# A recommendation model on one core: the product of GRU state and item moves from GpSimd to VectorE

## The chip, the cores and the metric

One core of a Trainium2 chip. The metric is the time of one execution on the device in microseconds (us), lower is better. Engines are named as the profile names them: PE (TensorE matmuls), PEld (its weight loads), DVE (VectorE), ACT (ScalarE), POOL (GpSimd), SP (SyncE, which issues most DMAs).

## The reference, cut to what matters

B = 1024 users, T = 100 history items of 128 numbers, hidden size 128, all in float32. A GRU runs over the history; an attention MLP scores each GRU state against the user's item; the scores are made a softmax over time; the pooled result weights a second recurrence (AUGRU); a last MLP gives one score a user.

```python
def gru_step(h, x_t):
    gi = x_t @ gru_Wih.T + gru_bih
    gh = h @ gru_Whh.T + gru_bhh
    r, z = sigmoid(i_r + h_r), sigmoid(i_z + h_z)
    n = tanh(i_n + r * h_n)
    return (1.0 - z) * n + z * h
keys = all the GRU states                       # B x T x 128
q = item_embedding, repeated for each t
feat = concatenate([keys, q, keys - q, q * keys], axis=-1)
score = mlp(feat, 512 -> 80 -> 40 -> 1, relu)
attn = softmax(where(mask == 1, score, -inf), axis=1)
pooled = einsum('bt,btd->bd', attn, keys)
# then: AUGRU over keys with weights from pooled, and the last MLP
```

## The kernel before, in words

The states are held transposed, 128 features on the partitions and users along the free axis. The 1024 users are two halves of 512 (`Half`), whose GRUs alternate. The first phase, `gru_phase`, loops over the 100 steps `s` and in each over the two halves. For one half it issues:

- `load(s + 2)` and `load_mask(s + 2)`: DMAs on SP, into pools of eight buffers each.
- `gru(s)`: the gate matmuls on PE (L363; each float32 matmul of 128x512 is two instructions), the sigmoids and the tanh on ACT (L375, L380, L394), and five operations on DVE: `u` (L383), the sum L393, and L396, L397, L398, the last of which writes the new state `hn`.
- `attend(s - 1)`: the first layer of the attention MLP for the state of the step before. The features `keys` and `q` are folded into the weights `wk` and into the constant `q0`; for `q * keys` the kernel forms `kq`, state times item, 128x512 (L429), in a pool `wp` of two buffers. PE multiplies `wk` by the state (L431) and `wkq` by `kq` (L432) into the same PSUM tile `pm`; DVE adds `q0` (L434, `f`), ACT applies the relu.
- `transpose(s - 1)`: four transposes on PE (L409), a copy to SBUF by ACT (L410), and every fourth step a DMA of the key tile `kt` (eight buffers).
- `attend_more(s - 1)`, once a step: the two later layers for both halves together (PE L618 into `px`, ACT L627); the scores go out by a small DMA (L445).
- `stage()`: pieces of the softmax, run in blocks of up to eight steps (PE L470, DVE L475 to L493, ACT L485).
- `history(s)`: the masked sum of the raw items, two operations on POOL (L350, L351).
- `pool(2, nc.gpsimd)`: for up to two keys of a finished softmax block, weight and add, two operations on POOL each (L525, L526), and one rescaling a block (L511).

The PSUM pool of `pm`, the transposes, `px` and softmax's scores (tag "a") has two buffers, that of the gates six. At the end of the phase come the last pooling, `weights`, `features` and `sort_weights` (L582 builds comparison masks on POOL).

The order on each engine is not simply that of the program text. The framework plans the whole phase beforehand with costs of its own: whenever an engine comes free in the plan, it takes, among the instructions whose inputs and buffers are ready in the plan, the one that comes first in the program. The order so found is fixed; on the chip each engine works through its own queue in that order and waits on semaphores.

The second phase, `augru_phase`, holds the AUGRU and the last MLP; it is planned apart from the first and has no part in the change.

Of the kernel before, what the change touches and what calls it, by code (L numbers as in the profile page):

```python
# [53 lines left out]
def kernel(ctx: ExitStack, tc: tile.TileContext, a: dict, out: bass.AP):  # L54
# [16 lines left out]
    nc = tc.nc  # L71
# [18 lines left out]
    item = const.tile([P, B], F32, name="item")  # L90
# [28 lines left out]
    def gru_phase(pools):  # L119
# [195 lines left out]
        class Half:  # L315
# [102 lines left out]
            def attend(self, t):  # L418

                i = self.i  # L420
                mv = wp.tile([P, HB], F32, name="mv", bufs=4)
                self.old, self.mv = self.mv, mv
                if t == T:
                    nc.gpsimd.memset(mv, 0.0)
                if t >= T:
                    return
                h = self.h[t]
                kq = wp.tile([P, HB], F32, name="kq")
                nc.gpsimd.tensor_mul(kq, h, item[:, self.cols])  # L429
                p = pa.tile([P, HB], F32, tag="a", name="pm")  # L430
                nc.tensor.matmul(p, lhsT=wk[i], rhs=h, start=True, stop=False)  # L431
                nc.tensor.matmul(p, lhsT=wkq[i], rhs=kq, start=False, stop=True)  # L432
                f = wp.tile([P, HB], F32, name="f")
                nc.vector.tensor_add(f, p, q0[:, self.cols])  # L434
                nc.scalar.activation(mv, f, AF.Relu)
# [453 lines left out]
```

## Time and profile before

| | us |
|---|---|
| median of three runs | 2664.23 (2659.52 to 2665.18) |
| the profiled execution's own time | 2684.05 |
| its span | 2681.6 |
| PE busy | 2434.5 (91%) |
| DVE busy | 1382.1 (52%) |
| ACT busy | 1215.7 (45%) |
| POOL busy | 1370.2 (51%) |
| GRU phase with its end | about 0 to 1912 |
| AUGRU phase | about 1912 to 2681 |

Busy shares are averages over the whole span: POOL is used mostly in the first phase. In the groups of the page, a row gives the line, the engine, the operation, what it writes and reads, shapes and count, then busy time and mean duration in ns, and last the idle time of the engine just before these instructions with what ended most of it. A timeline row gives start, duration, engine, line and operation; merged rows carry a count, and a bracket holds the idle time before and what ended it. The granted clock is the share of full speed that PE was given.

### The profile page before, as it was taken

How to read it: one execution, taken by the hardware profiler on the slowest of the kernel's cores; microseconds unless marked ns; L12 is line 12 of the kernel's file. 1: busy time of each engine (PE TensorE's matmuls, PEld its weight loads, DVE VectorE, ACT ScalarE, POOL GpSimd, SP SyncE). 2: the span in 40 equal slices, each digit the busy share in tenths (PEclk: the TensorE clock that was granted, in tenths of full speed). 3: DMA queues.
4: the chain of work that ended last, by engine and by line, in shares of the span. 5: the costliest groups of instructions: out<-in, count | busy, mean ns of one | idle time of the engine just before them, and what ended most of it. 6: DMA issues, size and time to landing. Idle time of an engine off the chain costs nothing. (4 is left out here: it accounts for less than half of the span.)

```text
span 2681.6 us, 25839 instructions
## 1 busy us (share of the span) xinstructions
PE 2434.5 (91%) x7688; PEld 1232.2 (46%) x7688; DVE 1382.1 (52%) x2530; ACT 1215.7 (45%) x2125; POOL 1370.2 (51%) x1215
## 2 busy tenths in 40 slices
PE   8999888898888888899888888897789999999998
PEld 3443333343333333344333333333444555667887
DVE  6644444544444444545444444454356666666664
ACT  3544444444444444444444444443234444455554
POOL 3457877565656767665656767667512111211220
PEclk9999999999999999999999999998799999999998
DMA  6323322212222222112222222111223233333331
GB/s 141 99 81 97 95 90 66 74 58 73 77 73 76 75 74 75 52 61 73 74 77 73 77 73 77 49 64 36 86 80 108 85 101 98 93 92 96 79 86 23
DMA packets 141655, 210.20 MB, mean 78 GB/s; under 512 B 29646, under 2 KB 75698, under 8 KB 141506
## 3 DMA queue, kind: packets, MB, share of 16 engines
q1 hardware_dynamic: 129410, 170.93, 20.7%
q0 software_dynamic: 12096, 37.54, 4.9%
q8 instruction: 62, 1.02, 0.2%
q14 instruction: 87, 0.71, 0.1%
HBM read 154.12 MB, written 53.87 MB: 78 GB/s over the span
## 5 line engine op out<-in xcount | busy, mean ns | idle before, releaser
L363 PE MATMUL ps<-x,wih 128*128 128x512 f32 x1200 | 603.2, 613 | 4.6 <-DMA x<-in_hist_x 4.6
L363 PE MATMUL ps<-hn,whh 128*128 128x512 f32 x1188 | 594.4, 609 | 0.0
L429 POOL TENSOR_TENSOR kq<-hn,item 128x512 f32<-128x512 f32 x200 | 254.5, 1278 | 559.1 <-DVE hn L398 540.5
L432 PE MATMUL pm<-kq,wkq 128*128 128x512 f32 x400 | 239.6, 684 | 190.2 <-POOL kq L429 190.1
L383 DVE SCALAR_TENSOR_TENSOR u<-ps,bhh,r 128x512 f32<-128x512 f32 x198 | 148.6, 750 | 506.2 <-ACT r L375 309.6
L101 POOL DMA_INDIRECT rows<-keys_d,idx x140 | 132.8, 949 | 535.9 <-PE pk L714 490.4
L363 PEld LDWEIGHTS ps<-hn,whh 128*128 128x128 f32 x1188 | 223.1, 195 | 326.8 <-issue 319.6
L410 ACT COPY kt<-pk 128x512 f32<-128x512 f32 x200 | 117.3, 586 | 517.2 <-PE pk L409 515.7
L363 PEld LDWEIGHTS ps<-x,wih 128*128 128x128 f32 x1200 | 221.7, 199 | 199.3 <-issue 197.9
L394 ACT ACTIVATE ps<-ps,bih 128x512 f32<-128x512 f32 x200 | 132.4, 662 | 321.6 <-DVE ps L393 317.9
L351 POOL TENSOR_TENSOR hist<-hist,xm 128x512 f32<-128x512 f32 x200 | 251.8, 1274 | 1.6
L434 DVE TENSOR_TENSOR f<-pm,q 128x512 f32<-128x512 f32 x200 | 136.7, 684 | 215.1 <-PE pm L432 215.0
L526 POOL TENSOR_TENSOR pooled<-pooled,kw 128x512 f32<-128x512 f32 x190 | 242.3, 1275 | 4.3
L350 POOL TENSOR_TENSOR xm<-x,m 128x512 f32<-128x512 f32 x200 | 229.4, 1162 | 22.9 <-DMA x<-in_hist_x 16.7
L432 PEld LDWEIGHTS pm<-kq,wkq 128*128 128x128 f32 x400 | 79.5, 210 | 300.1 <-POOL kq L429 223.6
L431 PE MATMUL pm<-hn,wk 128*128 128x512 f32 x400 | 206.9, 599 | 6.0 <-ACT kt L410 3.7
L396 DVE TENSOR_TENSOR d<-hn,ps 128x512 f32<-128x512 f32 x198 | 136.0, 687 | 138.5 <-ACT ps L394 137.6
L525 POOL TENSOR_TENSOR kw<-kt,e 128x512 f32<-128x512 f32 x190 | 196.8, 1052 | 1.7 <-DVE old L492 0.4
L409 PEld LDWEIGHTS pk<-ident,hn 128*128 128x128 f32 x800 | 112.6, 155 | 125.8 <-issue 116.8
L627 ACT ACTIVATE mv<-px,bx 41x512 f32<-41x512 f32 x202 | 137.9, 683 | 68.4 <-PE px L618 65.8
L375 ACT ACTIVATE r<-ps,brz 128x512 f32<-128x512 f32 x200 | 137.5, 688 | 67.7 <-PE ps L363 64.6
L743 DVE TENSOR_TENSOR ph<-ph,h 128x512 f32<-128x512 f32 (+22 forms) x198 | 94.6, 478 | 142.4 <-ACT ph L741 127.5
(139 smaller groups left out, 3608.7 us busy)
## 6 DMA issues: line engine op xcount, KB each, us to landing
x<-in_hist_x SPq DMA_DIRECT2D x212, 256.0 KB
keys_d<-kt SPq DMA_DIRECT2D x50, 1024.0 KB
m<-mask_d SPq DMA_DIRECT2D x200, 128.0 KB
at<-att_d SPq DMA_DIRECT2D x22, 256.0 KB
s_b<-mv SPq DMA_DIRECT2D x200, 2.0 KB
rows<-keys_d,idx POOLq DMA_INDIRECT x140
at<-att_d SPq DMA_DIRECT2D x8, 246.5 KB
at<-att_d SPq DMA_DIRECT2D x8, 236.0 KB
```

The source lines that it names most:

```text
L350: nc.gpsimd.tensor_mul(d, x, m)
L351: nc.gpsimd.tensor_add(acc, acc, d)
L363: nc.tensor.matmul(p, lhsT=w[:, g, :], rhs=v, start=(j == 0), stop=(j == len(parts) - 1),)
L375: nc.scalar.activation(r, pr, AF.Sigmoid, bias=brz[:, 0:1])
L383: nc.vector.scalar_tensor_tensor(out=u, in0=ph, scalar=bhh[:, 2:3], in1=r, op0=ALU.add, op1=ALU.mult,)
L429: nc.gpsimd.tensor_mul(kq, h, item[:, self.cols])
L431: nc.tensor.matmul(p, lhsT=wk[i], rhs=h, start=True, stop=False)
L432: nc.tensor.matmul(p, lhsT=wkq[i], rhs=kq, start=False, stop=True)
L434: nc.vector.tensor_add(f, p, q0[:, self.cols])
L525: eng.tensor_mul(d, k, w)
L526: eng.tensor_add(acc, acc, d)
L627: nc.scalar.activation(half.mv[r, :], p[r, :], AF.Relu, bias=bx[r, :])
```

## The change

`attend` forms `kq` on VectorE instead of GpSimd; nothing else in the text of the kernel differs. The planner makes its order anew.

```diff
                 h = self.h[t]
                 kq = wp.tile([P, HB], F32, name="kq")
-                nc.gpsimd.tensor_mul(kq, h, item[:, self.cols])
+                nc.vector.tensor_mul(kq, h, item[:, self.cols])
                 p = pa.tile([P, HB], F32, tag="a", name="pm")
                 nc.tensor.matmul(p, lhsT=wk[i], rhs=h, start=True, stop=False)
                 nc.tensor.matmul(p, lhsT=wkq[i], rhs=kq, start=False, stop=True)
```

## The prediction

> **What bounds the kernel now.** I read the page first (shares of the engines, then the costliest groups), then PE's waits, then a timeline of a few steps, then stretches of time. Lines of the page:
>
> ```profile
> span 2681.6 us, 25839 instructions
> PE 2434.5 (91%) x7688; PEld 1232.2 (46%) x7688; DVE 1382.1 (52%) x2530; ACT 1215.7 (45%) x2125; POOL 1370.2 (51%) x1215
> L429 POOL TENSOR_TENSOR kq<-hn,item 128x512 f32<-128x512 f32 x200 | 254.5, 1278 | 559.1 <-DVE hn L398 540.5
> L432 PE MATMUL pm<-kq,wkq 128*128 128x512 f32 x400 | 239.6, 684 | 190.2 <-POOL kq L429 190.1
> ```
>
> PE is busy 91% of the span. Nearly all of its idle time in the GRU phase stands in front of one line, L432, and one releaser ends it: the product kq on POOL, 190.1 us. The next three answers are PE's waits between 139 and 1770 us, the busy times of two stretches of the GRU phase and its end, and of one period of eight steps.
>
> ```profile
> PE pm L432 <- POOL kq L429: 169.0, 33, 7.5
> 100.00:1770.00 1670.00, 1500.94 (x4035) 655.03 (x4034) 794.89 (x1265) 757.12 (x1143) 1081.18 (x928) 0.94 0.23 74
> 1770.00:1912.00 142.00, 106.84 (x337) 51.85 (x336) 72.43 (x158) 54.12 (x90) 100.65 (x85) 0.89 0.12 44
> 1165.30:1315.50 150.20, 134.81 (x361) 58.90 (x360) 71.36 (x114) 67.66 (x103) 95.61 (x83) 0.93 0.22 71
> ```
>
> In a stretch row the columns after the length are PE, PEld, DVE, ACT, POOL, granted clock, DMA. POOL is busy only 1081 of 1670 us, and it idles 540.5 us waiting for hn: it is late not for want of time, but because kq stands in its queue behind bursts of `history` and `pool` work. The timeline shows a step without and one with such a wait (start, duration; in brackets the idle time before):
>
> ```profile
> 1005.61 1.02 PE L432 MATMUL pm<-kq,wkq 128*128 128x512 f32 x2
> 1006.55 0.69 DVE L398 TENSOR_TENSOR hn<-ps,d 128x512 f32<-128x512 f32 x1
> 1007.15 0.68 DVE L434 TENSOR_TENSOR f<-pm,q 128x512 f32<-128x512 f32 x1
> 1007.38 1.28 POOL L429 TENSOR_TENSOR kq<-hn,item 128x512 f32<-128x512 f32 x1 [7.32 <-DVE hn L398]
> 1007.77 1.88 PE L363 MATMUL ps<-hn,whh 128*128 128x512 f32 x4
> 1009.75 0.75 DVE L383 SCALAR_TENSOR_TENSOR u<-ps,bhh,r 128x512 f32<-128x512 f32 x1 [1.92 <-PE ps L363]
> 1012.92 1.02 PE L432 MATMUL pm<-kq,wkq 128*128 128x512 f32 x2
> 1013.75 0.69 DVE L398 TENSOR_TENSOR hn<-ps,d 128x512 f32<-128x512 f32 x1
> 1014.36 0.68 DVE L434 TENSOR_TENSOR f<-pm,q 128x512 f32<-128x512 f32 x1
> 1015.17 1.06 PE L618 MATMUL px<-mv,w 121*41 121x512 f32 x4
> 1018.48 0.75 DVE L383 SCALAR_TENSOR_TENSOR u<-ps,bhh,r 128x512 f32<-128x512 f32 x1 [3.44 <-ACT r L375]
> 1021.95 1.02 PE L432 MATMUL pm<-kq,wkq 128*128 128x512 f32 x2
> ```
>
> ```profile
> 612.12 1.27 POOL L429 TENSOR_TENSOR kq<-hn,item 128x512 f32<-128x512 f32 x1
> 613.44 2.08 PE L432 MATMUL pm<-kq,wkq 128*128 128x512 f32 x2 [7.39 <-POOL kq L429]
> 617.58 1.88 PE L363 MATMUL ps<-hn,whh 128*128 128x512 f32 x4
> 1197.75 2.08 PE L432 MATMUL pm<-kq,wkq 128*128 128x512 f32 x2 [2.36 <-POOL kq L429]
> ```
>
> The kq made from the hn of 1006.55 is read only at 1021.95, a step later, since `attend(s-1)` follows `gru(s)`. After a wait the two L432 matmuls take 2.08 us instead of 1.02: the wait also halves PE's clock for a while (granted on average 0.94 in the long stretch). From L432 to the whh matmuls it is 4.14 us there (613.44 to 617.58) against 2.16 (1005.61 to 1007.77): 1.98 us more.
>
> **What a step is without waits, and with.** Starts of px, one per step:
>
> ```profile
> 1107.53 1.06 PE L618 MATMUL px<-mv,w 121*41 121x512 f32 x4
> 1123.33 1.06 PE L618 MATMUL px<-mv,w 121*41 121x512 f32 x4
> 1165.34 1.06 PE L618 MATMUL px<-mv,w 121*41 121x512 f32 x4
> 1315.54 1.05 PE L618 MATMUL px<-mv,w 121*41 121x512 f32 x3
> ```
>
> An unhindered step takes 15.80 us, eight of them 126.4; the eight from 1165.34 take 150.20. That is 23.8 us lost per period, of which some 15.4 are waits for kq (2.36 above is one of three) and 8.4 the slow clock and what else follows.
>
> **The change, part by part.** *Removed from POOL:* 200 products of 1.278 us, 254.5 us. POOL's own time is worth nothing; what counts is that L432 no longer stands behind POOL's queue. *The waits:* 169.0 us in the 33 cases between 139 and 1770 us go: -169.0. *The clock:* 33 x 1.98 = 65 us go with them: -65 (bounds: 0, and by the period's ratio 8.4/15.4 x 169.0 = 92). The Trainium skill, in "TensorE: Matmul & The Clock Gate", section "What's actually happening", says that the clock falls to half after an idle window of some 3.4 us and rises after as long a busy one. By that, as an estimate, a wait would cost 1.7 us, 33 of them 56, and the sum would be 2444; the row of 1197.75 disagrees with it in one point, since there 2.36 us of idling were enough. *The end:* 190.1 - 169.0 = 21.1 us of waits lie almost all after 1770, where POOL is busy 100.65 of 142 us with pooling that must be done anyway; I take -5 (bounds 0 and -21).
>
> *Added to VectorE:* 200 products of two SBUF operands. The nearest rows are the same shape on VectorE at the end of the phase, the first of these, and a small product of softmax that met a POOL operation:
>
> ```profile
> L525 DVE TENSOR_TENSOR kw<-kt,e 128x512 f32<-128x512 f32 x8 | 5.5, 685 | 1.2 <-POOL pooled L526 1.2
> 1025.65 1.06 POOL L511 TENSOR_TENSOR pooled<-pooled,e 128x512 f32<-128x512 f32 x1 [1.07 <-ACT e L485]
> 1025.72 1.01 DVE L492 TENSOR_TENSOR old<-den,e 128x4 f32<-128x4 f32 x1
> ```
>
> So 0.685 us each, 137 us in all, if nothing is in the way. L492 has four columns, yet lasts 1.01 us, to within 0.02 us of the end of POOL's L511 (1026.71): a VectorE product of two SBUF operands waits out the POOL operation that it meets. A kq may so last up to 1.28 + 0.69 = 1.97 us. Where does it stand? kq can start when hn is done (1007.24), behind f (until 1007.83), and the next VectorE work of the GRU, u, starts at 1009.75: a gap of 1.92 us; in the other half f ends at 1015.04 and u starts at 1018.48, a gap of 3.44. Free, it is hidden (0.69 of 1.92); blocked in full it makes u 0.05 us late. A late u costs little by itself: the hn that follows is read by PE a step later. Where softmax shares the gap, the slip can reach f and through it px. I take +10 us (bounds 0 and 66, below). If the gap were gone, the 137 us would come on the path. *New wait:* kq needs a buffer (two of them) that the L432 two products earlier read; that ended at 1006.63, ahead of hn. Queued behind kq on VectorE are u of the other half and softmax's small operations; PE waits for both only by way of hn and f.
>
> *Queues it is moved past:* on POOL, `history` and `pool` no longer stand behind a kq that waits for hn, so x and mask buffers are freed earlier and SyncE issues those loads at other times. POOL's load per period falls from 95.61 to 95.61 - 16 x 1.278 = 75.2 us, 59% of 127: no bound. No DMA is added or removed.
>
> **Where the planner puts it.** Lines of a queue are not in program order, as two places show (L582 belongs to `sort_weights`, the last thing in the phase):
>
> ```profile
> 1856.06 1.56 POOL L582 TENSOR_SCALAR here<-ranks,rank 128x512 f32<-128x512 f32 x1 [4.10 <-PE ps L363]
> 1020.76 0.69 DVE L396 TENSOR_TENSOR d<-hn,ps 128x512 f32<-128x512 f32 x1 [0.73 <-ACT ps L394]
> 1021.36 0.18 DVE L475 TENSOR_TENSOR e<-pt,on 128x32 f32<-128x32 f32 x1
> 1021.68 0.68 DVE L397 TENSOR_TENSOR d<-ps,d 128x512 f32<-128x512 f32 x1
> ```
>
> Work that is ready is drawn ahead, over steps of the GRU on POOL and between two steps of one GRU on VectorE. So I expect kq in VectorE's gap right after its hn, a step before PE needs it, not where the program has it, after the next hn.
>
> **The sum**, against the median 2664.2: -169.0 - 65 - 5 + 10 = -229, so 2435 us. The profiled execution took 2684.05, 0.7% above the median; its waits are used as they stand.
>
> **Rivals.**
> (a) *Slower: kq stays in program order on VectorE.* Then it starts after the hn of the next step, and L432, for which PE was ready at 1005.61, starts at 1007.24 + 0.69 = 1007.93: 2.3 us late; in the other half 1014.44 + 0.69 = 15.13 against 12.92, 2.2. That is 4.5 us a step, 450 in 100 steps, against 239 won (169 + 65 + 5): 2664 - 239 + 450 = 2875, more if such waits halve the clock as at 1197.75. It decides when over 239/2.25 = 106 of the 200 stand so. L475 and L582 speak against it; for it speaks that no row shows a VectorE instruction drawn ahead by a whole step.
> (b) *POOL blocks VectorE on the path.* POOL without kq is busy about (1081 - 226)/1670 = 51% in the long stretch (226 for kq's share, 254.5 x 1670/1880), a hit waits 0.64 us on average: 0.33 x 200 = 66 us, if all of it came on the path; 2664 - 239 + 66 = 2491. Much the same comes if kq is put ahead of f: px starts 0.13 us after f's end (1015.04), so 0.69 us a step, 69 in all. The gaps speak against both. The rule of the Trainium skill that speaks against the change is this one: "SBUF — State Buffer", section "Who interferes with whom", has VectorE with two SBUF inputs and a reading GpSimd exclude each other for a whole instruction; the row of L492 agrees.
> (c) *Another wait takes over:* x loads, whose buffers wait for `history`, or key buffers that wait for `pool`. Half of the 239 would be left: 2545. For it: POOL still works in bursts, and a faster PE asks for x sooner. Against it: PE's matmuls waited for an x only once, at the start, with POOL more loaded than it will be:
>
> ```profile
> PE ps L363 <- DMA x<-in_hist_x: 4.6, 1, 4.6
> ```
>
>
> **How the numbers follow.** Main case (2395 to 2475) 0.60; (b) 0.18; (c) 0.13, of which 0.03 with the whole gain lost; (a) 0.07; better than 2395 0.02. The low end is 2664 - 169 - 92 - 8 = 2395. The high end, 2560, takes in (b) and the half loss of (c). Faster 0.90, within 0.2% (about what a measurement of this kernel can tell from no change) 0.03, slower 0.07.
>
> **What would show it.** Right: no wait of PE at L432 worth over 20 us in all, granted clock from 100 us on near 0.99, nearly every px 15.8 to 16.4 us after the last, kq at 0.69 to 1.97 us directly behind f or hn, and the phase after the GRU unchanged at some 770 us. Wrong: L432 waiting about 2 us for VectorE in each half step (a), px waiting for f (b), or L363 waiting for x and L409 for key buffers (c).

## The result, and the profile after

The changed kernel takes 2404.24 us (median; 2402.62 to 2407.18) against 2663.4: a ratio of 0.903, interval 0.9014 to 0.9046. It is 259 us faster; 229 were forecast, and 2404 lies in the main case (2395 to 2475), at its fast end.

From the page of the changed kernel, the engines and three of the costliest groups:

```profile
PE 2349.1 (98%) x7688; PEld 1200.1 (50%) x7688; DVE 1557.9 (65%) x2730; ACT 1211.0 (50%) x2125; POOL 1173.1 (49%) x1015
```

```profile
L432 PE MATMUL pm<-kq,wkq 128*128 128x512 f32 x400 | 204.4, 592 | 0.0
L429 DVE TENSOR_TENSOR kq<-hn,item 128x512 f32<-128x512 f32 x200 | 198.4, 992 | 0.9
L351 POOL TENSOR_TENSOR hist<-hist,xm 128x512 f32<-128x512 f32 x200 | 267.2, 1351 | 2.5
```

PE's longest waits in the changed kernel (total us, count, longest):

```profile
PE px L618 <- ACT kt L410: 17.5, 14, 8.2
PE pw L589 <- DVE att L538: 11.3, 1, 11.3
```

L432 stood idle 190.1 us before and stands idle 0.0 now. VectorE is 176 us busier and POOL 197 less. The product itself lasts 0.992 us on average, not 0.685, and POOL's `history` sum 1.351 us instead of 1.274: the two engines get in each other's way. What that costs on the path is looked at below, with POOL made quiet.

The same 87 steps of the GRU phase, px to px, before and after (length, PE, PEld, DVE, ACT, POOL, clock, DMA share, GB/s):

```profile
139.20:1766.00 1626.80, 1457.74 (x3913) 636.27 (x3912) 773.52 (x1231) 733.14 (x1108) 1057.61 (x907) 0.94 0.23 74
```

```profile
129.20:1525.70 1396.50, 1388.31 (x3913) 609.32 (x3912) 932.56 (x1406) 728.11 (x1108) 890.87 (x732) 1.00 0.27 87
```

The same 3913 PE instructions take 230.3 us less. PE's idle time fell from 169.06 to 8.19 us (160.9), its busy time by 69.4 us, with the granted clock up from 0.94 to 1.00. A step (1396.5/87) takes 16.05 us, close to the 15.80 of an unhindered one: the phase is now bound by PE. The timeline of one step shows kq where it was expected:

```profile
803.68 1.02 PE L432 MATMUL pm<-kq,wkq 128*128 128x512 f32 x2
804.45 0.69 DVE L398 TENSOR_TENSOR hn<-ps,d 128x512 f32<-128x512 f32 x1
805.05 0.68 DVE L434 TENSOR_TENSOR f<-pm,q 128x512 f32<-128x512 f32 x1
805.65 0.86 DVE L429 TENSOR_TENSOR kq<-hn,item 128x512 f32<-128x512 f32 x1
805.93 1.06 PE L618 MATMUL px<-mv,w 121*41 121x512 f32 x4
809.24 0.75 DVE L383 SCALAR_TENSOR_TENSOR u<-ps,bhh,r 128x512 f32<-128x512 f32 x1 [2.72 <-ACT r L375]
812.18 1.02 PE L432 MATMUL pm<-kq,wkq 128*128 128x512 f32 x2
```

kq follows f, and VectorE still idles 2.72 us before u. PE's own order is, but for two instructions in the first steps, that of the kernel before, over all 7688.

### The profile page after: what moved, and what is told of

The parts are those of the page before. It is cut to its first block, busy times and chain, and to the rows that moved or that the text cites. A ratio compares the mean times of both kernels' runs of the same rounds, so it can differ in the third digit from the quotient of the medians.

```text
span 2400.8 us, 25461 instructions
## 1 busy us (share of the span) xinstructions
PE 2349.1 (98%) x7688; PEld 1200.1 (50%) x7688; DVE 1557.9 (65%) x2730; ACT 1211.0 (50%) x2125; POOL 1173.1 (49%) x1015
## 5 line engine op out<-in xcount | busy, mean ns | idle before, releaser
L363 PE MATMUL ps<-x,wih 128*128 128x512 f32 x1200 | 582.5, 595 | 4.2 <-DMA x<-in_hist_x 4.2
L351 POOL TENSOR_TENSOR hist<-hist,xm 128x512 f32<-128x512 f32 x200 | 267.2, 1351 | 2.5
L350 POOL TENSOR_TENSOR xm<-x,m 128x512 f32<-128x512 f32 x200 | 244.5, 1239 | 39.2 <-DMA x<-in_hist_x 34.9
L511 POOL TENSOR_TENSOR pooled<-pooled,e 128x512 f32<-128x512 f32 x25 | 26.3, 1051 | 463.2 <-ACT e L485 463.2
L526 POOL TENSOR_TENSOR pooled<-pooled,kw 128x512 f32<-128x512 f32 x190 | 247.6, 1303 | 6.6
L525 POOL TENSOR_TENSOR kw<-kt,e 128x512 f32<-128x512 f32 x190 | 209.2, 1119 | 1.8 <-DVE old L492 0.6
L432 PE MATMUL pm<-kq,wkq 128*128 128x512 f32 x400 | 204.4, 592 | 0.0
L429 DVE TENSOR_TENSOR kq<-hn,item 128x512 f32<-128x512 f32 x200 | 198.4, 992 | 0.9
L435 ACT ACTIVATE mv<-f 128x512 f32<-128x512 f32 x200 | 126.0, 630 | 114.3 <-DMA s_b<-mv 59.1
L741 ACT ACTIVATE ph<-ph,bh 128x512 f32<-128x512 f32 (+22 forms) x200 | 97.2, 486 | 125.9 <-PE ph L727 125.6
L393 DVE TENSOR_TENSOR ps<-ps,u 128x512 f32<-128x512 f32 x200 | 140.0, 700 | 20.9 <-PE ps L363 0.5
```

Of the source, the lines that this page charges most:

```text
L350: nc.gpsimd.tensor_mul(d, x, m)
L351: nc.gpsimd.tensor_add(acc, acc, d)
L363: nc.tensor.matmul(p, lhsT=w[:, g, :], rhs=v, start=(j == 0), stop=(j == len(parts) - 1),)
L393: nc.vector.tensor_add(pi, pi, u)
L429: nc.vector.tensor_mul(kq, h, item[:, self.cols])
L525: eng.tensor_mul(d, k, w)
```

## The experiments

Chips and executions differ by up to 1% (the kernel before took 2663.8 us in one set and 2684.1 in another), so a run is read by its ratio to the kernel before beside it. The changed kernel has 0.903 in the result, and 0.9047 (0.9035 to 0.906) and 0.9029 (0.9017 to 0.9042) in two such sets. The set with kq first in rank, kq late by dependence, kq twice and POOL quiet has no run of it; there the mean of the three, 0.9035, stands for it.

**kq on POOL, first in rank.** A theory for the gain: kq was late because of its place in POOL's fixed queue, not because POOL is slow.

```diff
-                nc.gpsimd.tensor_mul(kq, h, item[:, self.cols])
+                with tc.high_priority():
+                    nc.gpsimd.tensor_mul(kq, h, item[:, self.cols])
```

> kq stays on GpSimd as in the kernel before; only its place in the plan changes: it is given the highest priority, so the planner takes it ahead of all history and pooling work that is ready. Theory (the waits came from kq's place in POOL's queue, not from the engine's speed or load): PE's waits at L432 fall from 190 us to under 20 and the time to 2400 to 2440. Rival (POOL is too slow or too loaded, and the gain comes from VectorE's 0.69 us against 1.28): the waits stay above 100 us and the time above 2550.

Ratio 1.0004 (0.9995 to 1.0014): nothing moved. Its wait of PE for kq (this kernel's lines are one higher):

```profile
PE pm L433 <- POOL kq L430: 190.3, 38, 7.5
```

And in its timeline POOL's queue from one kq to the next, with 14.9 us of the other work, cut here, between the end of the first and the last row (1058.34 - 1042.20 - 1.26):

```profile
1042.20 1.26 POOL L430 TENSOR_TENSOR kq<-hn,item 128x512 f32<-128x512 f32 x1
1043.42 1.26 POOL L527 TENSOR_TENSOR pooled<-pooled,kw 128x512 f32<-128x512 f32 x1
...
1057.12 1.26 POOL L351 TENSOR_TENSOR hist<-hist,xm 128x512 f32<-128x512 f32 x1
1058.34 1.26 POOL L430 TENSOR_TENSOR kq<-hn,item 128x512 f32<-128x512 f32 x1
```

The burst stayed where it was, and the order of PE, VectorE, ScalarE and POOL came out the same, instruction by instruction, as in the kernel before. Either the rank did not put the burst there or the edit did not reach the planner's choice; the run does not show which. It could not tell place from speed, since it did not change the place.

**kq on POOL, bursts cut up.** The next run changed the order itself, with order edges on POOL alone:

```diff
-                nc.gpsimd.tensor_mul(kq, h, item[:, self.cols])
+                last_kq[:] = [nc.gpsimd.tensor_mul(kq, h, item[:, self.cols])]
...
-                nc.gpsimd.tensor_mul(d, x, m)
+                behind_kq(nc.gpsimd.tensor_mul(d, x, m))   # issued after last_kq
...
```

> kq on GpSimd as in the kernel before, but each operation of history and of pooling may be issued only after the last kq that stands ahead of it in the program text (an order edge on the same engine, no wait), so that POOL's bursts are cut into pieces of at most 8 operations between two kq. The earlier run with a high priority left POOL's order as it was. Theory (kq comes late only because bursts stand ahead of it in the fixed queue): PE's waits at L432 fall below 40 us and the time to 2400 to 2450, a ratio of 0.90 to 0.92. Rival (POOL cannot do this work in time at all): waits above 100 us, ratio above 0.96.

The multiplications on GpSimd in `pool()` (but for that of the first key) are held behind `last_kq` in the same way. PE, VectorE and ScalarE keep the order of the kernel before but for at most six instructions each, so POOL's order is what the run changes. Ratio 0.9099 (0.9082 to 0.9115): 242 us (2684.05 - 2442.45) against the changed kernel's 255 (2684.05 - 2429.32) in the same set, 95% of the gain with kq still on GpSimd at 1.277 us. PE's wait for kq in this kernel:

```profile
PE pm L445 <- POOL kq L442: 4.0, 2, 3.8
```

POOL's queue in its timeline, from one kq to the next:

```profile
1009.85 1.27 POOL L442 TENSOR_TENSOR kq<-hn,item 128x512 f32<-128x512 f32 x1 [3.90 <-DVE hn L411]
1011.08 1.16 POOL L363 TENSOR_TENSOR xm<-x,m 128x512 f32<-128x512 f32 x1
...
1016.78 1.27 POOL L543 TENSOR_TENSOR pooled<-pooled,kw 128x512 f32<-128x512 f32 x1
1018.01 1.26 POOL L442 TENSOR_TENSOR kq<-hn,item 128x512 f32<-128x512 f32 x1
```

And the engines' busy time in a stretch of the length of the 87 steps:

```profile
129.00:1526.00 1397.00, 1383.12 (x3886) 607.76 (x3887) 781.01 (x1227) 730.98 (x1100) 1054.07 (x898) 1.00 0.27 86
```

At most 6.9 us of other work stand between these two kq. POOL does as much as before in that stretch (1054 us), with the clock at 1.00. So the loss came from the order of POOL's queue: with a better order, the engine's speed and load cost next to nothing. Why the plan lets such bursts stand ahead of kq (whether it reckons POOL's operations too short, for instance) was not tried.

**kq on VectorE, but late.** Rival (a) of the prediction, made on purpose by a dependence on the hn of the next step:

```diff
...                                                     # for t < T - 1
+                    z = wp.tile([P, 1], F32, name="z")
+                    nc.vector.tensor_scalar_mul(z, self.h[t + 1][:, 0:1], 0.0)
-                nc.vector.tensor_mul(kq, h, item[:, self.cols])
+                    nc.vector.scalar_tensor_tensor(out=kq, in0=h, scalar=z,
+                        in1=item[:, self.cols], op0=ALU.add, op1=ALU.mult)
```

> kq on VectorE, but made to depend on the hn of the next step (one column of it times zero is added to the state, one more 128x1 operation a product), so that it stands where the program text has it. Theory (the place in the queue decides): L432 waits about 2.3 us in each half step and the time is 2404 + 450 = about 2850, up to 3250 if such waits halve PE's clock. Rival (moving to VectorE gains wherever it stands): 2404 to 2430.

Ratio 0.9148 (0.9129 to 0.9166): only some 30 us dearer than kq in the gap (0.9148 - 0.9035 = 0.011 of 2680.59). Both expectations missed, the theory's by far and the rival's by little. PE's wait for kq in this kernel is small:

```profile
PE pm L444 <- DVE kq L432: 8.6, 26, 1.5
```

PE's order in its timeline shows why:

```profile
813.85 1.02 PE L363 MATMUL ps<-x,wih 128*128 128x512 f32 x2
814.71 1.88 PE L363 MATMUL ps<-hn,whh 128*128 128x512 f32 x4
816.58 1.12 PE L444 MATMUL pm<-kq,wkq 128*128 128x512 f32 x2
```

The planner moved the second attention matmul (L444 here) behind the first gate matmuls of the next half, where kq is ready or nearly so. Holding it in its place tells whether that is the reason:

```diff
+                        if last_mm:                     # the L432 ahead in the text
+                            tc.add_manual_dep(op.ins, last_mm[0].ins.name, ...)   # each gate matmul
```

> The kernel of e2 (kq on VectorE, made to depend on the hn of the next step) with one thing more: on TensorE the gate matmuls of a half may be issued only behind the L432 that stands ahead of them in the program text (an order edge on the same engine, no wait). In e2 the planner had moved L432 behind the next half's first gate, and PE waited only 8.6 us for kq in all. Theory (the predicted price of rival (a) failed because the planner moved L432 with kq): with L432 held in place PE waits some 2 us in nearly every half step, 2430 + 450 = about 2850 on this scale, up to 3250 if PE's clock halves. Rival (a late kq is cheap in any order): below 2550.

2870.3 us, ratio 1.0776 (1.0757 to 1.0796): slower than before, and 5 us from the 2875 that the prediction gave for rival (a). In the kernel before and in the changed one PE already keeps the order that the edge asks for, so the edge alone should cost nothing (it was not run without the late kq). PE's longest waits in it:

```profile
PE pm L456 <- DVE kq L444: 149.0, 127, 4.7
PE px L642 <- ACT kt L422: 97.2, 97, 2.9
PE pm L455 <- ACT kt L422: 70.7, 87, 11.1
```

And one late kq in its timeline:

```profile
806.80 0.69 DVE L410 TENSOR_TENSOR hn<-ps,d 128x512 f32<-128x512 f32 x1
807.53 0.15 DVE L443 TENSOR_SCALAR z<-hn 128x1 f32<-128x1 f32 x1
807.72 0.75 DVE L444 SCALAR_TENSOR_TENSOR kq<-hn,z,item 128x512 f32<-128x512 f32 x1
808.52 1.12 PE L456 MATMUL pm<-kq,wkq 128*128 128x512 f32 x2
```

The loss is spread. Against the changed kernel beside it, PE idles 319 us more in the GRU phase: 149 us at L456, and 168 at px and L455, which both wait for ACT's copy `kt`. It is also busy 147 us longer for the same matmuls, at a clock of 0.94 instead of 0.99. The prediction's 450 us were 200 waits of some 2.25 us at L432 alone; here there are 127 of 1.2 us, since the planner moved L455 and the transposes as well. That the total comes within 5 us of 2875 is therefore in part luck. The place decides, on PE as on POOL: the same product on the same engine is worth 229 us or costs 207.

**kq twice on VectorE**, by doubling the line:

> The product kq is formed twice in a row on VectorE, 200 more products of 0.69 to 1.84 us, some 140 to 198 us of VectorE time. Theory (the gap before u covers VectorE's work, and hn is needed only a step later): 2404 to 2430. Rival (VectorE's time lies on the path): 2404 + 140 to 198, that is 2540 to 2600.

Ratio 0.9207 (0.919 to 0.9224), about 46 us more than the changed kernel ((0.9207 - 0.9035) x 2680.59). The groups of the two products:

```profile
L430 DVE TENSOR_TENSOR kq<-hn,item 128x512 f32<-128x512 f32 x200 | 238.4, 1192 | 6.0
L429 DVE TENSOR_TENSOR kq<-hn,item 128x512 f32<-128x512 f32 x200 | 204.4, 1022 | 0.8
```

And PE's longest wait in this kernel:

```profile
PE px L619 <- ACT kt L410: 46.2, 15, 9.7
```

A second product adds over 200 us of VectorE time and costs 46, more than theory said and far less than the rival: the gap seems to have room for one product, and only in part for two. How the second one's slip reaches px was not followed.

**POOL made quiet** (this kernel's lines are three lower):

```diff
-                nc.gpsimd.tensor_mul(d, x, m)
-                nc.gpsimd.tensor_add(acc, acc, d)
...
-                    else:
+                    elif eng is not nc.gpsimd:
```

> The changed kernel without history's two operations a step and without the pooling that runs on GpSimd (its output leaves out the masked history sum and most of the pooled keys), so that POOL reads almost nothing beside kq. Theory (VectorE's product waits out the POOL operation it meets, and this is hidden): kq falls from 0.992 us on average to 0.69, the steps in the middle stay 15.8 to 16.34 us, and the time falls only by what the end of the phase waits for POOL, to 2375 to 2404. Rival (the collisions cost time on the path): the steps get shorter and the time falls below 2350.

Ratio 0.9013 (0.8994 to 0.9031), against 0.9029 and 0.9047 of the changed kernel. Its group of the product, and then its engines' busy time in the same 87 steps, px to px:

```profile
L426 DVE TENSOR_TENSOR kq<-hn,item 128x512 f32<-128x512 f32 x200 | 138.0, 690 | 0.8
```

```profile
149.25:1535.15 1385.90, 1385.90 (x3913) 608.65 (x3912) 859.56 (x1406) 736.57 (x1108) 22.56 (x21) 1.00 0.23 76
```

And PE's longest wait in this kernel:

```profile
PE pt L467 <- DMA s_b<-mv: 20.1, 3, 18.9
```

With POOL still, kq takes 0.690 us: the 0.302 us above that in the changed kernel are POOL's. Taking them away buys little: the 87 steps take 1385.9 us against 1396.5, with PE busy all the time, so the collisions cost 10.6 us there at most. The ratio alone hides this. The end of the phase is 16.7 us shorter without the pooling, but one wait of 18.9 us early on, where the score DMAs stand behind mask loads in SP's queue, takes most of both back. The Trainium skill, "SBUF — State Buffer", section "Who interferes with whom", has VectorE with two SBUF inputs and a reading GpSimd shut each other out; the kq of 0.992 and 0.690 us agree with it.

**The end of the phase.** In the changed kernel the longest of px's waits, 8.2 us, lies there:

```profile
1588.16 0.32 SPq L549 DMA_DIRECT2D rlen<-rlen_d  x1
1589.05 14.16 SPq L445 DMA_DIRECT2D s_b<-mv  x6
1594.36 0.63 ACT L435 ACTIVATE mv<-f 128x512 f32<-128x512 f32 x1 [11.09 <-DMA s_b<-mv]
1599.06 1.94 PE L618 MATMUL px<-mv,w 121*41 121x512 f32 x4 [8.24 <-ACT kt L410]
```

Score DMAs pile up behind the rlen load on SP, ACT waits for them 11.09 us, and px behind ACT 8.24. Two edits go at that, and a third at the PSUM buffer for which px's weight loads wait.

```diff
-                rlen = xp.tile([P, HB], F32, tag="x", name="rlen")      # own_rlen
+                rlen = mid.tile([P, HB], F32, tag="once", name="rlen")
...
-                nc.sync.dma_start(out=rlen, ...)                        # rlen_queue
+                nc.gpsimd.dma_start(out=rlen, ...)
...
-        ps = ... bufs=6 ...    pa = ... bufs=2 ...                      # banks_5_3
+        ps = ... bufs=5 ...    pa = ... bufs=3 ...
```

The base beside the first two edits to run:

> The changed kernel once more, unaltered, as the base for the two variants beside it: a ratio of 0.903 to the kernel before.

Own buffers for rlen:

> The changed kernel, with the buffers of rlen taken from the pool mid, idle by then, instead of from that of x. In the changed kernel's trace the rlen load stands on SP ahead of six score DMAs and waits for the last history operation; ACT's mv waits 11.1 us for those DMAs, and PE's px 8.2 us behind it. Theory (an SP queue order holds the end of the GRU phase): that wait goes, 8 to 14 us less than the changed kernel, ratio 0.898 to 0.900. Rival (POOL's own work holds the end): no change, 0.903.

Five and three PSUM buffers:

> The changed kernel with five PSUM buffers for the gates and three for the attention tiles, instead of six and two. px waits in each step until the copy of the transposes has freed its buffer (weight load idle 0.76 us, matmuls about 0.3). Theory (that buffer sets the 15.8 us of a step): 0.2 to 0.5 us less a step, ratio 0.885 to 0.896. Rival (the gates need six, or PE has no other gap): 0.903 or above.

The base beside the last edit:

> The changed kernel unaltered, as the base for the run beside it: ratio 0.903 to 0.905 to the kernel before.

The rlen loads on GpSimd's queue:

> The changed kernel with the two rlen loads issued from GpSimd's queue instead of SP's; the planned order of PE, VectorE and ScalarE stays the same instruction by instruction. Theory (at the end of the phase SP's queue holds six score DMAs behind an rlen load that waits for history on POOL, and PE's px 8.2 us behind them): that wait goes, 8 to 12 us less than the changed kernel beside it, a ratio to it of 0.995 to 0.997. Rival (POOL's own work holds the end): no change.

Own buffers for rlen: 0.9056 (0.9043 to 0.9068); five and three PSUM buffers: 0.906 (0.9048 to 0.9073); the changed kernel beside them 0.9047 (0.9035 to 0.906). Neither helps. In the first, PE, VectorE and ScalarE keep the order of the changed kernel and the old wait is gone, but a new one of much the same size stands behind VectorE:

```profile
PE pm L431 <- DVE f L434: 7.8, 1, 7.8
```

Its timeline shows where it comes from:

```profile
1612.24 9.02 DVE L429 TENSOR_TENSOR kq<-hn,item 128x512 f32<-128x512 f32 x1
1619.45 1.25 POOL L526 TENSOR_TENSOR pooled<-pooled,kw 128x512 f32<-128x512 f32 x1
1620.69 1.99 POOL L582 TENSOR_SCALAR here<-ranks,rank 128x512 f32<-128x512 f32 x1
1621.30 0.62 DVE L434 TENSOR_TENSOR f<-pm,q 128x512 f32<-128x512 f32 x1
```

One kq lasts 9.02 us. POOL runs eight pooling operations back to back over that time (the L526 here is the last), and kq ends 0.56 us after them, as if it had waited out all eight and not one. So a product on VectorE can be held far longer than the 1.97 us that the prediction took as the most, and here it lies on the path. This run therefore does not speak against SP's queue as the cause of the old wait.

In the second, the 87 steps are 5.4 us shorter (1391.3 against 1396.7 in the changed kernel beside it), which is 0.06 us a step and not the 0.2 to 0.5 of the theory, and PE waits for VectorE's `d`, which reads a gate's buffer, above all once in the first steps:

```profile
PE ps L363 <- DVE d L397: 10.5, 3, 7.3
```

The rlen loads on GpSimd's queue, with PE's, VectorE's and ScalarE's order unchanged: 2394.39 us against 2404.91 of the changed kernel beside it, ratios to the kernel before of 0.8995 (0.8983 to 0.9008) and 0.9029 (0.9017 to 0.9042). That beats both kernels, by 10.5 us over the changed one. One kq lasts 6.43 us in its trace, but PE does not wait behind it. px's waits fell from 18.0 to 8.2 us:

```profile
PE px L618 <- ACT kt L410: 8.2, 12, 4.2
```

## Why the prediction was right

**The accounts.** First matmuls of the AUGRU phase on the state, which bound the GRU phase, before and after:

```profile
L727 PE MATMUL pr<-h,wr x396: 275/419/1061, 1941.9 to 2665.9; 128*128 128x512 f32 x22, 128*128 128x493 f32 x8, 128*128 128x472 f32 x8, 128*128 128x451 f32 x8
```

```profile
L727 PE MATMUL pr<-h,wr x396: 275/419/593, 1682.5 to 2385.1; 128*128 128x512 f32 x22, 128*128 128x493 f32 x8, 128*128 128x472 f32 x8, 128*128 128x451 f32 x8
```

They start 259.4 us earlier, the whole of the gain. (The AUGRU phase so begins some 20 to 30 us later than the 1912 in the table of the time before.) The gain splits into 230.3 in the 87 steps of the middle, 10.0 before them (139.2 against 129.2) and 19.1 behind (1941.9 - 1766.0 = 175.9 against 1682.5 - 1525.7 = 156.8).

- *The waits at L432*, forecast -169: right in kind; the idle time of the middle fell by 160.9, as 8.2 us of other waits remain.
- *The clock*, forecast -65: 69.4 less busy time for the same instructions. The 65 us at 1.98 us a wait were nearer than the 56 us estimated by the Trainium skill's page "TensorE: Matmul & The Clock Gate", section "What's actually happening". That this one price, read after a wait of 7.39 us, comes near the mean of 33 waits from 1.05 to 7.51 us is in part luck: four of them were followed by no slow pair. The row below this list, from the kernel before, has a wait as long as that of 1197.75, with 1.12 us for the two matmuls instead of 2.08, so the length of a wait alone does not tell whether the clock falls. Also, eight steps of the changed kernel take 128.4 us on average, not 126.4, so the 8.4 us of the prediction's period were some 2 too many.
- *VectorE's product*, +10: at most 8.2 of idle time, all that PE has left in the middle; without POOL's collisions the middle is 10.6 us shorter. The length was forecast well (0.685 alone, 0.33 of hindrance by rival (b)'s working; measured 0.690 and 0.302) and so was the cover: a gap that one product fits in.
- *The end*, -5: mis-sized, 19.1 us. POOL's pooling there was taken as fixed work that would hold PE anyhow; it did not. Of 20.9 us of waits for kq after 1766 none is left; PE's idle time fell by 13.2 us and its busy time by 5.9. The new hold is SP's queue (8.2 us); moving the rlen loads off it won another 10 us.
- *The start*, not in the sum: 10.0 us. PE idled 4.9 us less there and was 5.1 us shorter busy. Only 0.2 us of its waits there were for kq; 5.7 us stood behind ACT's copy `kt` and are gone, where the planned order of the first steps differs a little. The forecast had no term for this.

```profile
597.29 1.12 PE L432 MATMUL pm<-kq,wkq 128*128 128x512 f32 x2 [2.37 <-POOL kq L429]
```

So the 30 us by which the sum fell short are 14 at the end, 10 at the start and 6 in the middle (230.3 against 169 + 65 - 10).

*The planner's place for kq* was right. Of the rivals, the total of (a) came out for a PE order that is held fast (2870 measured), but not its terms: a third of the loss stood at L432, the rest in waits for `kt` and in the slow clock. It left out that the planner moves L432 along with kq; then a late kq costs only 30 us. (b)'s collisions came nearly in full (0.302 x 200 = 60 us of 66), and all but some 10 us were hidden; the kernel with rlen's own buffers shows that a long one can land on the path. Something of (c)'s kind, another wait that takes over, came at the end of the phase alone. The explanation that kq stood behind bursts in POOL's queue is now shown, by the run that cut them up.

## What to carry to other kernels

When an engine that is half idle holds up the bound one, look at what stands ahead of the late instruction in its queue before asking how fast the engine is: here order edges on the slow engine won 95% of what a faster engine did. A waiting matmul costs its wait and the slow clock after it, here 69 us on top of 161. And the price of a late input is only as good as the assumption that nothing else is reordered: say which order is held. A product with two SBUF operands on VectorE stays exposed to POOL: it is mostly hidden here, but one was held for 9.02 us.

## What was not expected of the hardware

The AUGRU phase, which the change does not touch, takes one of two lengths: 724.0 us in the profile before and 702.6 in that after (the rows above), but 727.6 for the changed kernel in another set. The length seems to go with the set, each of which ran on another chip, and not with the execution: the nine executions of the kernel before took 2679 to 2686 us in that other set, and 2660 to 2665 in the set of the rlen loads, where the changed kernel's phase takes 702.7. The group of the same matmuls in the set with 727.6, and then VectorE's wait in that phase:

```profile
L727 PE MATMUL pr<-h,wr x396: 275/419/1061, 1682.8 to 2410.4; 128*128 128x512 f32 x22, 128*128 128x493 f32 x8, 128*128 128x472 f32 x8, 128*128 128x451 f32 x8
```

```profile
DVE u L739 <- issue: 21.1, 15, 11.0
```

In the long form VectorE stands idle with nothing to wait for that the profile shows; the profile of 702.6 has no such wait. That is likely the 20 us by which the profiled execution before stood above its median, whose other executions left no trace. The cause is open.
